# Two Sobel layers on shifted instead of normalized data, and weight centring moved into the attention

## The chip, the cores and the metric

The kernel runs on one core of a Trainium2 chip. The metric is the device time of one execution in microseconds (us), the median of several runs. A profile of one further execution gives the duration of every instruction on the core's engines: TensorE (PE in the profile, its weight loads PEld), VectorE (DVE), ScalarE (ACT), GpSimd (POOL) and SyncE (SP, which here issues transfers). Each engine works through its own queue in order; semaphores make it wait for the others.

## The reference

The input x has 256 rows, 256 columns and 32 channels, in float32. Four residual layers follow one another, each `x = x + layer(gn(x))`, where `gn` is a group norm with 16 groups of 2 channels over the whole image and no parameters.

- Layer 0: attention over an axis of length one, so that the softmax is 1 and only a layer norm, value and gate projections, their product and an output projection remain.
- Layers 1 and 2: a Sobel layer. `pooled` is the 3x3 mean of the normalized image, divided at the borders by the number of pixels that exist; `grad_x` and `grad_y` are the two 3x3 Sobel filters of it with zero padding; the result is `sqrt(grad_x^2 + grad_y^2 + 1e-6)`.
- Layer 3: a two-layer recurrent cell with group-normalized gates, which runs over the 256 columns, with the 256 rows as a batch.

For the change two facts count. A Sobel filter is linear and the group norm is `(x - mean) / deviation`, one mean and deviation per channel group. So the division may be done behind the filter, before or within the squares. The mean must be taken away ahead of it, since the zero padding makes the borders see it.

## The kernel before

**Layout.** The image lies in SBUF with 128 partitions = 4 columns x 32 channels, 64 blocks of 4 columns, 256 rows along the free axis. Work goes by pairs of blocks: `pair(t, k)` is 128 partitions x 512 elements, for k = 0 to 31. `xa` and `xb` are two such images; layer 1 reads `xa` and writes `xb`, layer 2 the reverse.

**Stages.** Input and transposes; group norm; layer norm; attention (L307 to L372); group norm (L376); first Sobel layer (L546); group norm (L548); second Sobel layer (L549); group norm and final weights (L559 to L561); the recurrence, which takes about three quarters of the time and has a plan of its own.

**Group norm** (L155). Per-partition means and variances of all pairs (`bn_stats`, L512, and `bn_aggr`, L158) are averaged over the partitions of a group by small products with a constant matrix; further products with a junk result (`busy`) keep TensorE at work meanwhile. A square root (L173), a reciprocal (L175) and one operation more (L177) give `scale` and `bias`.

**One pair in a Sobel layer.** A layer is a list of parts with due times, `every` apart from one pair to the next; all parts of all pairs are sorted by due time, and each engine gets its instructions in that order, with nothing reordered afterwards. The parts:

- `normalize` (L416): ScalarE writes scale * x + bias twice, into PSUM (`xp`) and SBUF (`xn`).
- `twos` (L423), `threes` (L432): VectorE adds neighbours along the rows, u[i] = xn[i] + xp[i+1], then pp = u[i] + xp[i+2]. `ends` (L426): ScalarE makes the two border values, 1.5 times u.
- `fours` (L437): VectorE, v = pp[i] + pp[i+1]. `difference` (L445): GpSimd, dh = pp[i] - pp[i+2]. `smooth` (L441): GpSimd, sh = v[i] + v[i+1]. dh and sh go into rings of 8 blocks (4 pairs).
- `centre` (L452, L462) and `edges` (L492): TensorE applies the filter across the columns. The centre is a product with the pair's own blocks, 128 rows and 128 columns of weights; the edges take one column from the block before and one from the block behind, with weights of 64 rows x 64 columns, into the two column halves. This is done for dh (`pg1`) and for sh (`pg0`). A float32 product shows as two records.
- `square` (L498) on ScalarE, twice; `total` (L502, ss) on VectorE; `root` (L506) on ScalarE; `residual` (L509) and `statistics` (L512) on VectorE.

The PSUM tiles `pg0` and `pg1` have three buffers each and `xp` two, eight banks in all. `pg1` holds dh's filter, then its square, then the root, until the residual has been added.

**Between the pairs.** Each `statistics` may be followed by one callback from a list. In layer 1 these are the centring steps of the recurrent weights (L634): `wc` and `bc` have their mean over each gate's 128 columns taken away, by reductions on VectorE (L644, L648) and subtractions on GpSimd (L651). In layer 2 they are five weight products (L658), which take a `pg1` buffer each. The loads of `wc`, `bc` and other weights are issued on SP's queue when `RecurrentWeights` is made, behind the attention (L374, L600 to L612).

**Attention.** For each of 32 pairs: eight value products and eight gate products on TensorE (L318), eight sigmoids on ScalarE (L333), eight multiplications on VectorE (L336), one `statistics` (L355), and a projection of eight products with 32 columns of weights each (L342), whose result GpSimd adds to the image (L352).

Of the kernel before, what the change touches and what calls it, by code (L numbers as in the profile page):

```python
# [61 lines left out]
def net_kernel(  # L62
# [120 lines left out]
    avg = big2.tile([P, KS, KS, J], F32, name="avg")  # L183
# [3 lines left out]
    spread = big2.tile([P, KS * J, C], F32, name="spread")  # L187
# [118 lines left out]

    stats = new_stats()  # L307
    with tc.tile_pool(name="at", bufs=3) as atp, tc.tile_pool(
# [48 lines left out]
        with tc.manual_schedule():  # L357
            together((), [(0, j) for j in range(J)])
            together((), [(1, j) for j in range(2)])
            for i in range(NST):  # L360
                for u in (2 * i, 2 * i + 1):
                    if i >= 3 and u % 2:
                        statistics(i - 3)
                    together([(u, 0), (u, 1)], [(u + 1, 2), (u + 1, 3)])
                    together([(u, 2), (u, 3)], [(u + 2, 0), (u + 2, 1)])
                if i >= 1:
                    project(i - 1)
            table(AF.Sqrt, one)
            for i in range(NST - 1, NST):
                project(i)  # L370
            for i in range(NST - 3, NST):
                statistics(i)  # L372
    lw = ctx.enter_context(tc.tile_pool(name="lw", bufs=1))
    rw = RecurrentWeights(tc, lw, ident, bout4, w_lat, b_lat, w_cell, b_cell, w_out)  # L374
    with tc.tile_pool(name="ps_gn", bufs=1, space=PSUM) as ps_gn:
        gn = group_norm(stats, ps_gn, 7, 12)  # L376
# [8 lines left out]
    def sobel_layer(src, dst, scale, bias, between):  # L385
# [24 lines left out]
        def normalize(k):  # L410
            for key, t in (
                ("xp", ps_c.tile([P, 2, S], F32, name="xp")),
                ("xn", sp.tile([P, 2, S], F32, name="xn")),
            ):
                v[key, k] = t
                nc.scalar.activation(  # L416
                    flat(t), pair(src, k), AF.Identity, scale=scale, bias=bias
                )

        def twos(k):  # L420
            u = v["u", k] = sp.tile([P, 2, S - 1], F32, name="u")
            xn, xp = v.pop(("xn", k)), v["xp", k]
            nc.vector.tensor_add(u, xn[:, :, 0 : S - 1], xp[:, :, 1:S])  # L423

        def ends(k):
            nc.scalar.mul(  # L426
                pps[k % 2][:, :, 1 : S + 1 : S - 1], v["u", k][:, :, 0 : S - 1 : S - 2], 1.5
            )

        def threes(k):  # L430
            u, xp = v.pop(("u", k)), v.pop(("xp", k))
            nc.vector.tensor_add(pps[k % 2][:, :, 2:S], u[:, :, 0 : S - 2], xp[:, :, 2:S])  # L432

        def fours(k):
            pp = pps[k % 2]
            w = v["v", k] = sp.tile([P, 2, S + 1], F32, name="v")
            nc.vector.tensor_add(w, pp[:, :, 0 : S + 1], pp[:, :, 1 : S + 2])  # L437
# [9 lines left out]
        def centre(k, which):  # L447
            pg = v["pg", which, k] = ps_s.tile([P, 2, S], F32, name=f"pg{which}")
            k0 = K_SOBEL + 5 * which
            b = 2 * k % RING  # L450
            if 0 < k < NST - 1:
                nc.tensor.matmul(  # L452
                    flat(pg),
                    lhsT=kt[:, k0 + 1, :],
                    rhs=flat(along[which][:, ring(k), :]),
                    start=True,
                    stop=False,
                )
                return
            for i in range(2):  # L460
                m = 3 if 2 * k + i == 0 else 4 if 2 * k + i == NB - 1 else 1
                nc.tensor.matmul(  # L462
                    pg[:, i, :],
                    lhsT=kt[:, k0 + m, :],
                    rhs=along[which][:, b + i, :],
                    start=i == 0,
                    stop=False,
                )

        def edges(k, which):  # L470

            pg = v["pg", which, k]
            k0 = K_SOBEL + 5 * which
            sides = []
            for m, first, rows, cols in (
                (0, 2 * k - 1, slice(Q, P), slice(0, Q)),
                (2, 2 * k + 1, slice(0, Q), slice(Q, P)),
            ):
                blocks = [(n, n - first) for n in (first, first + 1) if 0 <= n < NB]
                parts = []  # L480
                if len(blocks) == 2 and (first + 1) % RING:
                    b = first % RING
                    parts.append((flat(along[which][rows, b : b + 2, :]), flat(pg[cols])))
                else:
                    for n, i in blocks:
                        parts.append((along[which][rows, n % RING, :], pg[cols, i, :]))
                sides.append([(kt[rows, k0 + m, cols], rhs, out) for rhs, out in parts])
            while any(sides):
                for side in sides:
                    if side:  # L490
                        w, rhs, out = side.pop(0)
                        nc.tensor.matmul(out, lhsT=w, rhs=rhs, start=False, stop=not side)  # L492

        def square(k, which):
# [3 lines left out]
            nc.scalar.activation(sq, pg, AF.Square)  # L498
# [12 lines left out]
        def statistics(k):  # L511
            nc.vector.bn_stats(stats[:, k, :], pair(dst, k))  # L512

        every = 4.0
        parts = [
            (-1.45, normalize, ()),
            (0.0, twos, ()),
            (0.66, ends, ()),
            (0.66, threes, ()),
            (1.32, fours, ()),  # L520
            (1.4, difference, ()),
            (2.05, smooth, ()),
            (2.6 + 4.0, centre, (1,)),
            (3.46 + 4.0, centre, (0,)),
            (0.3 + 8.0, edges, (1,)),
            (1.35 + 8.0, edges, (0,)),
            (1.5 + 8.0, square, (1,)),
            (2.5 + 8.0, square, (0,)),
            (3.2 + 8.0, total, ()),
            (0.0 + 12.0, root, ()),  # L530
            (1.98 + 12.0, residual, ()),
            (2.6 + 12.0, statistics, ()),
# [5 lines left out]
        with tc.manual_schedule():  # L538
            for _, k, part, args in todo:
                part(k, *args)  # L540
                if part is statistics and between:
# [4 lines left out]
    stats = sobel_layer(xa, xb, *gn, rw.centring())  # L546
    with tc.tile_pool(name="ps_n", bufs=1, space=PSUM) as ps_n:
        gn = group_norm(stats, ps_n, 3, 12)  # L548
    stats = sobel_layer(xb, xa, *gn, rw.products())  # L549
# [41 lines left out]
class RecurrentWeights:  # L591


    def __init__(self, tc, lw, ident, bout4, w_lat, b_lat, w_cell, b_cell, w_out):
        self.nc = nc = tc.nc
        self.ident, self.bout4 = ident, bout4

        self.wc = lw.tile([P, L, 2, G], F32, name="wc")
        for l in range(L):
            nc.sync.dma_start(out=self.wc[:, l], in_=w_cell[l].rearrange("(k p) m -> p k m", p=P))  # L600
        self.wm = lw.tile([P, L * 2 * 4], F32, name="wm")

        self.bc = lw.tile([KX, L, G], F32, name="bc")
        nc.gpsimd.memset(self.bc, 0.0)
        nc.sync.dma_start(out=self.bc[C : C + 1], in_=b_cell.rearrange("(o l) m -> o l m", o=1))
        self.bm = lw.tile([KX, L * 4], F32, name="bm")

        self.lat = lw.tile([KX, H], F32, name="lat")
# [25 lines left out]
    def centring(self):  # L634
# [21 lines left out]
        return [lambda ps, p=out[i : i + 2]: [f() for f in p] for i in range(0, len(out), 2)]  # L656
# [441 lines left out]
```

## Time and profile before

| | us |
|---|---|
| median of 3 runs (2587.21 to 2589.66) | 2588.59 |
| the profiled execution | 2584.07 |
| its span, first to last instruction | 2582.1 |
| attention, about 107 to 320.8 | 213.8 |
| first Sobel layer, from L158 at 322.83 to L158 at 470.11 | 147.28 |
| second Sobel layer, to L158 at 615.72 | 145.61 |
| VectorE busy in the two layers | 130.87 and 127.64 |
| TensorE busy in the two layers | 142.50 and 140.16 |
| ScalarE busy in the two layers | 105.44 and 106.85 |
| GpSimd busy in the two layers | 96.05 and 82.55 |

In a line of the costliest groups, the line of the code, the engine and the operation are followed by `out<-in` with the names of the tiles, the shapes, the count, the busy time, the mean of one in ns, and behind the second bar the idle time of the engine just ahead of them with what ended it. In a line of the timeline stand the start and the duration in us, then the same names; a bracket at the end is the engine's idle time ahead of it and what ended it. Durations may overlap the next start by a little[...]; the distance of two starts is what an operation costs its queue.

### The profile page before, as it was taken

To read this page: it belongs to the slowest core of one execution; us is meant where nothing else is said; L and a number is where in the kernel's file an instruction comes from. 1 tells how busy PE (TensorE), PEld (TensorE's weight loads), DVE (VectorE), ACT (ScalarE), POOL (GpSimd) and SP (SyncE) were. 2 spreads that over 40 slices of the span, in tenths; PEclk is the share of its full clock that TensorE was granted. 3 is DMA by queue.
4 is the path that set the end of the run, shared out by engine and by line. 5 is a ranking of instruction groups with operands and counts; after the bars stand their busy time and mean duration, and the time that the engine had idled before them with its cause. 6 is when DMAs were issued, how large, how long until landed. Compare 5 with 4: busy or idle time off the path is not lost.

```text
span 2582.1 us, 40860 instructions
## 1 busy us (share of the span) xinstructions
PE 2530.7 (98%) x11181; PEld 1041.5 (40%) x11181; DVE 2317.7 (90%) x6735; ACT 2282.5 (88%) x6948; POOL 1284.0 (50%) x1292
## 2 busy tenths in 40 slices
PE   7999999998999999999999999999999999999997
PEld 4433333433344444444444444444444444444442
DVE  6788789896999999999999999999999999999997
ACT  5677667675999999999999999999999999999996
POOL 3211267563555555555555555555555555555553
PEclk9899999998999999999999999999999999999999
DMA  4000000002001001010101010100101010100000
GB/s 149 1 1 1 1 18 1 1 1 49 1 6 24 14 13 22 5 21 5 22 5 21 5 21 5 24 10 18 22 5 21 5 22 5 21 5 5 5 5 10
DMA packets 110870, 38.53 MB, mean 15 GB/s; under 512 B 74868, under 2 KB 107797, under 8 KB 110632
## 3 DMA queue, kind: packets, MB, share of 16 engines
q1 hardware_dynamic: 108452, 34.54, 6.2%
q8 instruction: 91, 1.49, 0.2%
q14 instruction: 147, 1.20, 0.2%
q10 hardware_dynamic: 1380, 0.99, 0.1%
q0 software_dynamic: 800, 0.30, 0.1%
HBM read 10.63 MB, written 8.39 MB: 7 GB/s over the span
## 4 chain that ended last, share of the span: by engine, by line
PE 94%; DVE 3%; ACT 1%; DMA 1%; POOL 0%; issue 0%; DVEq 0%; SPq 0%; ACTq 0%; POOLq 0%
PE zz L916 36%; PE zz L911 17%; PE zz L884 9%; PE pt L968 5%; PE pv L318 5%; PE pg L492 4%; PE pg L452 3%; PE zz L881 3%; PE pg L342 2%; PE pt L964 2%; PE px L1013 1%; PE pg L318 1%; PE pc L262 1%; PE px L1003 1%; PE pb L283 1%; DMA nat<-in_x_dram 1%
## 5 line engine op out<-in xcount | busy, mean ns | idle before, releaser
L932 POOL TENSOR_TENSOR rs<-ve,mhalf 128x4 f32<-128x4 f32 x1024 | 1032.1, 1008 | 921.9 <-DVE ve L929 921.9
L916 PE MATMUL zz<-wc,hT 128*128 128x512 f32 x2040 | 1058.6, 606 | 0.7 <-DVE hT L974 0.7
L905 ACT ACTIVATE ga<-zz,rs 128x128 f32<-128x128 f32 x3072 | 972.8, 377 | 39.2 <-POOL rs L932 9.7
L929 DVE TENSOR_REDUCE ve<-sq 128x4 f32<-128x516 f32 x1024 | 703.9, 687 | 27.9 <-ACT sq L924 7.1
L924 ACT ACTIVATE sq<-zz 128x512 f32<-128x512 f32 x1024 | 629.7, 615 | 37.0 <-PE zz L916 14.4
L911 PE MATMUL zz<-wc,hT 128*128 128x512 f32 x1024 | 524.2, 594 | 0.0
L916 PEld LDWEIGHTS zz<-wc,hT 128*128 128x128 f32 x2040 | 328.3, 190 | 398.1 <-DVE c L960 167.6
L905 ACT ACTIVATE go<-zz,rs 128x128 f32<-128x128 f32 x1024 | 394.0, 385 | 0.0
L952 DVE TENSOR_TENSOR c<-ga 128x128 f32<-128x128 f32 x1024 | 299.9, 293 | 62.0 <-ACT ga L905 40.3
L960 DVE TENSOR_TENSOR c<-c,fc 128x128 f32<-128x128 f32 x1020 | 288.4, 283 | 9.0
L956 DVE TENSOR_TENSOR fc<-ga,c 128x128 f32<-128x128 f32 x1020 | 292.5, 287 | 2.9 <-ACT ga L905 2.9
L884 PE MATMUL zz<-fx,xt 32*128 32x512 f32 x2048 | 265.7, 588 | 0.0
L336 DVE TENSOR_TENSOR o<-pv,sg 128x512 f32<-128x512 f32 x256 | 158.1, 681 | 42.4 <-PE pg L318 37.7
L968 PEld LDWEIGHTS pt<-ident,c 128*128 128x128 f32 x512 | 70.9, 139 | 285.5 <-DVE c L960 277.2
L971 ACT ACTIVATE th<-c 128x128 f32<-128x128 f32 x512 | 166.2, 325 | 0.4 <-DVE c L960 0.4
L333 ACT ACTIVATE sg<-pg 128x512 f32<-128x512 f32 x256 | 138.5, 599 | 30.7 <-PE pg L318 25.8
L971 ACT ACTIVATE th<-pt 128x128 f32<-128x128 f32 x512 | 146.0, 285 | 19.4 <-PE pt L968 19.4
L911 PEld LDWEIGHTS zz<-wc,hT 128*128 128x128 f32 x1024 | 161.0, 197 | 2.8 <-issue 0.5
L974 DVE TENSOR_TENSOR hT<-pt,th 128x128 f32<-128x128 f32 x512 | 146.3, 286 | 15.8 <-ACT th L971 15.7
L318 PE MATMUL pv<-xb,wv 32*128 32x512 f32 x512 | 156.2, 619 | 0.0
L980 DVE COPY hT<-pt 128x128 f32<-128x128 f32 x512 | 145.5, 284 | 8.9 <-PE pt L968 8.8
L964 PEld LDWEIGHTS pt<-ident,go 128*128 128x128 f32 x512 | 71.5, 140 | 202.9 <-ACT go L905 202.9
(169 smaller groups left out, 2986.6 us busy)
## 6 DMA issues: line engine op xcount, KB each, us to landing
xt<-xa SPq DMA_DIRECT2D x256, 64.0 KB, 2.0
nat<-in_x_dram SPq DMA_DIRECT2D x16, 512.0 KB, 7.9
out_dram<-st SPq DMA_DIRECT2D x252, 32.0 KB, 1.7
wc<-in_L_conv_W_cell_dram SPq DMA_DIRECT2D x2, 512.0 KB, 4.6
kt<-in_consts_dram ACTq DMA_DIRECT2D x1, 704.0 KB, 7.0
kg<-in_consts_dram ACTq DMA_DIRECT2D x1, 128.0 KB
wv<-in_L_conv_Wv_dram POOLq DMA_DIRECT2D x4, 32.0 KB, 5.4
wg<-in_L_conv_Wg_dram POOLq DMA_DIRECT2D x4, 32.0 KB, 6.4
```

What stands on the lines that cost most here:

```text
L318: nc.tensor.matmul(ps, lhsT=w[rows, half * P : (half + 1) * P], rhs=mn, start=True, stop=True)
L884: nc.tensor.matmul(v["zz", l, h, t], lhsT=inputs.of(t, r), rhs=fx[r, :], start=False, stop=l == 0 and t == 0,)
L905: nc.scalar.activation(dst, gates(x, g), func, scale=scale)
L911: nc.tensor.matmul(get("zz"), lhsT=v["hT", 0, t][:, seqs], rhs=wc[:, l, 0, :], start=False, stop=t == 0)
L916: nc.tensor.matmul(get("zz"), lhsT=v["hT", l, t - 1][:, seqs], rhs=wc[:, l, 1, :], start=False, stop=True,)
L924: nc.scalar.activation(sqs[l, h, t % 2][:, :, 0:H], four(get("zz")), AF.Square, scale=float(H**-0.5))
L929: nc.vector.tensor_reduce(ve, sqs[l, h, t % 2], AX.X, ALU.add)
L932: nc.gpsimd.tensor_tensor(rs, get("ve"), inputs.mhalf, ALU.pow)
L952: nc.vector.tensor_mul(c, gates(get("ga"), 0), gates(get("ga"), 2))
L956: nc.vector.tensor_mul(fc, gates(get("ga"), 1), get("c"))
L960: nc.vector.tensor_add(c, c, get("fc"))
L971: nc.scalar.activation(th, get("pt")[:, 1, 0:P] if turned else get("c"), AF.Tanh)
```

## The change

- `normalize` becomes `convert`: ScalarE writes x - 1.5 mean into `xp` alone, and `twos` adds the plain `src` to it. A sum of one plain value and two such values is a sum of three less 3 means. `ends` has -0.75 mean as bias. `scale` and its reciprocal are made by `deviation`, behind the first `twos`, and go into `square` as a scale.
- `fours` moves from VectorE to GpSimd.
- `centre` and `edges` become `mixed`: for each column half, products with all 128 rows of weights and 64 columns, one for the pair's own blocks and one for the neighbours; the two halves alternate.
- All due times are new; `every` goes from 4.0 to 3.44.
- The group norm ahead of a Sobel layer moves into the layer (`shift`), with 16 junk products behind its last small product instead of 12.
- The loads of `wc` and `bc` are issued ahead of the attention, once the tiles `avg` and `spread`, now in a pool of their own, are free. The 32 centring steps are emitted one behind each pair of the attention instead of two behind each of the first 16 pairs of layer 1. The remaining weights are loaded as before (`rest`).

```diff
+    means.close()
+    cells = ctx.enter_context(tc.tile_pool(name="cells", bufs=1))
+    rw = RecurrentWeights(tc, cells, w_cell, b_cell)
+    centring = rw.centring()
...
                 if i >= 1:
                     project(i - 1)
+                if centring:
+                    centring.pop(0)()
...
-    def sobel_layer(src, dst, scale, bias, between):
+    def sobel_layer(src, dst, moments, before, after, between):
...
-        def normalize(k):
-            for key, t in (
-                ("xp", ps_c.tile([P, 2, S], F32, name="xp")),
-                ("xn", sp.tile([P, 2, S], F32, name="xn")),
-            ):
-                v[key, k] = t
-                nc.scalar.activation(
-                    flat(t), pair(src, k), AF.Identity, scale=scale, bias=bias
-                )
+        def shift():
...
+            nc.vector.bn_aggr(mv, moments)
+            busy(before)
+            nc.tensor.matmul(pm[:, 0:1], lhsT=kg[:, K_GN, :], rhs=mv[:, 0:1], start=True, stop=True)
+            busy(2)
+            nc.scalar.mul(m15, pm[:, 0:1], -1.5)
+            nc.scalar.mul(m75, pm[:, 0:1], -0.75)
...
+            nc.tensor.matmul(pm[:, 1:2], lhsT=kg[:, K_GN, :], rhs=q, start=True, stop=True)
+            busy(after)
+
+        def deviation():
+            nc.scalar.activation(std, v.pop("pm")[:, 1:2], AF.Sqrt, bias=gn_eps)
+            nc.vector.reciprocal(scale, std)
+
+        def convert(k):
+            xp = v["xp", k] = ps_c.tile([P, 2, S], F32, name="xp")
+            nc.scalar.activation(flat(xp), pair(src, k), AF.Identity, bias=m15)
 
         def twos(k):
             u = v["u", k] = sp.tile([P, 2, S - 1], F32, name="u")
-            xn, xp = v.pop(("xn", k)), v["xp", k]
-            nc.vector.tensor_add(u, xn[:, :, 0 : S - 1], xp[:, :, 1:S])
+            nc.vector.tensor_add(
+                u, src[:, 2 * k : 2 * k + 2, 0 : S - 1], v["xp", k][:, :, 1:S]
+            )
...
-            nc.vector.tensor_add(w, pp[:, :, 0 : S + 1], pp[:, :, 1 : S + 2])
+            nc.gpsimd.tensor_add(w, pp[:, :, 0 : S + 1], pp[:, :, 1 : S + 2])
...
+        def mixed(k, which):
+
             pg = v["pg", which, k] = ps_s.tile([P, 2, S], F32, name=f"pg{which}")
             k0 = K_SOBEL + 5 * which
...
+            for side in range(2):
+                cols = slice(side * Q, (side + 1) * Q)
                 parts = []
...
+                for d in (side - 1, side):
+                    m = 1 + d
+                    blocks = [n for n in (2 * k + d, 2 * k + 1 + d) if 0 <= n < NB]
+                    whole = len(blocks) == 2 and (blocks[0] + 1) % RING
+                    if whole and (d or 0 < k < NST - 1):
+                        b = blocks[0] % RING
+                        parts.append((kt[:, k0 + m, cols], flat(along[which][:, b : b + 2, :]), flat(pg[cols])))
+                        continue
...
             while any(sides):
-                for side in sides:
+                for i, side in enumerate(sides):
                     if side:
-                        w, rhs, out = side.pop(0)
-                        nc.tensor.matmul(out, lhsT=w, rhs=rhs, start=False, stop=not side)
+                        w, rhs, dst = side.pop(0)
+                        first = len(side) == count[i] - 1
+                        nc.tensor.matmul(dst, lhsT=w, rhs=rhs, start=first, stop=not side)
...
-            nc.scalar.activation(sq, pg, AF.Square)
+            nc.scalar.activation(sq, pg, AF.Square, scale=scale)
...
-        every = 4.0
+        every = 3.44
         parts = [
-            (-1.45, normalize, ()),
-            (0.0, twos, ()),
-            (0.66, ends, ()),
-            (0.66, threes, ()),
-            (1.32, fours, ()),
-            (1.4, difference, ()),
-            (2.05, smooth, ()),
-            (2.6 + 4.0, centre, (1,)),
-            (3.46 + 4.0, centre, (0,)),
-            (0.3 + 8.0, edges, (1,)),
-            (1.35 + 8.0, edges, (0,)),
-            (1.5 + 8.0, square, (1,)),
-            (2.5 + 8.0, square, (0,)),
-            (3.2 + 8.0, total, ()),
-            (0.0 + 12.0, root, ()),
-            (1.98 + 12.0, residual, ()),
-            (2.6 + 12.0, statistics, ()),
+            (-0.72, convert, ()),
+            (0.00, twos, ()),
+            (2.77, threes, ()),
+            (2.77, ends, ()),
+            (4.40, fours, ()),
+            (5.57, difference, ()),
+            (7.15, smooth, ()),
+            (10.90, mixed, (1,)),
+            (11.97, square, (1,)),
+            (12.75, mixed, (0,)),
+            (12.85, square, (0,)),
+            (14.29, total, ()),
+            (14.79, root, ()),
+            (16.34, residual, ()),
+            (17.10, statistics, ()),
         ]
...
-    stats = sobel_layer(xa, xb, *gn, rw.centring())
...
-    stats = sobel_layer(xb, xa, *gn, rw.products())
+    stats = sobel_layer(xa, xb, stats, 7, 16, [])
+    stats = sobel_layer(xb, xa, stats, 3, 16, rw.products())
```

## The prediction

> **What bounds the kernel now.** I first cut the span into stages by the moments at which statistics are aggregated (L158): the attention ends near 320.8 us, the first Sobel layer runs from 322.83 to 470.11 (147.28 us), the second from there to 615.72 (145.61 us), and what follows, the recurrence, isn't touched. The chain of waits is almost all TensorE (94%), which misleads for the Sobel layers, so I read them from the queues. VectorE's timeline over one step of the first layer (columns: start, duration, engine, line, operation):
>
> ```profile
> 424.37 0.68 DVE L423 TENSOR_TENSOR u<-xn,xp 128x510 f32<-128x510 f32 x1
> 425.16 0.68 DVE L432 TENSOR_TENSOR pp<-u,xp 128x508 f32<-128x508 f32 x1
> 425.97 0.69 DVE L437 TENSOR_TENSOR v<-pp 128x514 f32<-128x514 f32 x1
> 426.58 0.68 DVE L509 TENSOR_TENSOR xb<-xa,pg 128x512 f32<-128x512 f32 x1
> 427.30 0.69 DVE L512 BATCH_NORM_STATS2 stats<-xb 128x6 f32<-128x512 f32 x1
> 427.91 0.67 DVE L502 TENSOR_TENSOR ss<-sq,pg 128x512 f32<-128x512 f32 x1
> 428.50 0.68 DVE L423 TENSOR_TENSOR u<-xn,xp 128x510 f32<-128x510 f32 x1
> ```
>
> Six operations, no idle time in brackets: VectorE sets the step of 4.13 us, the distance of the two u rows. The starts show more than the durations: an operation that reads what the one before it wrote starts 0.72 to 0.81 us after it (u to pp 0.79, pp to v 0.81, xb to stats 0.72), an independent one after 0.59 to 0.61 (v to xb, stats to ss, ss to u).
>
> Next, the other engines. TensorE, where it runs freely (339.17, 340.13, 341.08, 341.99, then 342.94), gives 0.96, 0.95, 0.91 and 0.95 to the four parts of a pair: 3.77 us. ScalarE waits 0.86 us each step for L502. GpSimd has one slow row and one that tells why:
>
> ```profile
> L445 POOL TENSOR_TENSOR dh<-pp 128x512 f32<-128x512 f32 x64 | 98.7, 1542 | 100.0 <-DVE pp L432 75.3 <-ACT xp L416 15.5 <-ACT pg L498 4.7
> L441 POOL TENSOR_TENSOR sh<-v 128x512 f32<-128x512 f32 x64 | 66.3, 1036 | 0.0
> ```
> ```profile
> 393.02 1.55 POOL L445 TENSOR_TENSOR dh<-pp 128x512 f32<-128x512 f32 x1 [0.41 <-DVE pp L432]
> 397.45 1.25 POOL L445 TENSOR_TENSOR dh<-pp 128x512 f32<-128x512 f32 x1 [0.71 <-DVE pp L432]
> 401.27 1.55 POOL L445 TENSOR_TENSOR dh<-pp 128x512 f32<-128x512 f32 x1 [0.41 <-DVE pp L432]
> ```
>
> The difference takes 1.55 us where it runs 0.66 us beside VectorE's v (L437), the one operation with both inputs in SBUF, and 1.25 where, started late, it shares only 0.36 us with it. That leaves 1.03, what sh takes.
>
> Last, the tail of the first layer, where nothing lies between the sum, the root and the residual:
>
> ```profile
> 463.67 0.67 DVE L502 TENSOR_TENSOR ss<-sq,pg 128x512 f32<-128x512 f32 x1
> 465.10 0.69 DVE L509 TENSOR_TENSOR xb<-xa,pg 128x512 f32<-128x512 f32 x1 [0.76 <-ACT pg L506]
> 465.82 0.69 DVE L512 BATCH_NORM_STATS2 stats<-xb 128x6 f32<-128x512 f32 x1
> ```
>
> From ss to xb VectorE needs 1.43 us, 0.76 of them idle. In the steady step above it had u, pp and v to do there.
>
> **The change part by part.** *VectorE loses v.* By starts that is 0.81 us of 4.13. But the new order matters more than the count. The due times, modulo 3.44, give VectorE: u(n) 0.00, ss(n-4) 0.53, xb(n-4) 2.58, pp(n) 2.77, stats(n-4) 3.34. ss and xb are now neighbours, and the root stands between them. An engine works through its queue in order, so the 1.43 us of the tail come into every step: u to ss 0.60, ss to xb 1.43, xb to pp 0.61, pp to stats 0.60, stats to u 0.61, together 3.85 us. If nothing else is slower, the step goes from 4.13 to 3.85, not to the 3.44 written in the code.
>
> *ScalarE* loses xn (0.80 us). Its queue is root(n-4), square 1 and square 0 of n-3, convert(n+1), ends(n). A second loop runs through it: ss to root 0.72, root to square 0.65, square to square 0.52, to convert 0.48, convert to u 0.80 (duration 0.77 and the hand-over), u to ss 0.60: 3.77. Just under 3.85, so hidden; it is what comes next if VectorE's loop were shorter.
>
> *GpSimd* gains fours (514 elements, two inputs). The Trainium skill speaks against this (GPSIMD Engine Reference, § 4.1 Engine selection): elementwise additions belong on VectorE, GpSimd being some 2x slower. By that rule, three times twice the 0.70 of v, GpSimd would need 4.2 us per step and set the pace, giving back the gain and 4 us more. The rows say less: 1.04 for sh, and dh falls to 1.03 since v no longer runs on VectorE (the page's § 1, contention with two SBUF inputs, agrees with the 1.25 row). I take 3 x 1.04 = 3.1; with dh left at 1.55 it is 3.6; with L352's in-place 1.27 for fours, 3.3. All below 3.85.
>
> *TensorE*: eight 128x64x512 products instead of two full and four quarter ones. L342's sixteen records on four column tiles take four slots of 0.43 us (weight loads at 316.26, 316.69, 317.12), so column tiles run side by side; two at a time, 16 records take 8 slots: 3.42 us. If the changes of tile shape cost the 0.35 us between that and 3.77 (TensorEngine Tiling (Array Packing), § Key Properties, says a change of mode drains the array), they are gone; otherwise 3.77 remains. Neither reaches 3.85.
>
> *Step and fill.* I follow the queues from the aggregation, t = 0. Mean ready 1.50 (as 322.83 to 324.33), m15 and m75 0.4, convert 0.77, so u(0) at 2.75 instead of 4.89; the deviation follows beside it. In the fill GpSimd counts: three operations per pair from 4.3, dh(1) ends at 9.4, sh(1) at 10.4, then the last product 0.9, square 0.6. Square 0 of pair 0 stands ahead of convert(4) in ScalarE's queue: u(4) at 12.7, ss(0) at 13.3. Then 27 steps of 3.85 to ss(27) at 117.25. Behind it pp(31) ends at 2.73, the three GpSimd operations at 5.86, four products 1.7 us each at 10.9, square, sum, root, residual, statistics 3.6: 14.5. A layer is 131.75 us. The first saves 147.28 - 131.75 = 15.5. The second has the weight products between its steps; today their steps (4.9, 4.73, 4.71, 4.35, 4.67) exceed 4.13 by 2.7 in all, and since two sums of 0.66, their waits and four copies (0.72) now fall into tighter loops, I put 2.5: 145.61 - 134.25 = 11.4.
>
> *Centring moves into the attention.* One of 32 steps behind each pair: six reductions (0.67 each) and two scalings on VectorE, 24 subtractions (0.60) on GpSimd. The place is just behind four gated products, where VectorE idles 1.22 us of 6.69 for TensorE:
>
> ```profile
> 225.31 2.48 DVE L336 TENSOR_TENSOR o<-pv,sg 128x512 f32<-128x512 f32 x4 [1.22 <-PE pg L318]
> ```
>
> So a reduction is hidden, and costs 0.6 where the gap is missing: at the first pair only, where sixteen products run without a gap (106.89 for 9.65 us). With no cover at all it would be 8 x 0.6 = 5. Its loads leave SP's empty queue near 103 us; the first reduction, and all gated products queued behind it, would wait for them if they took over 8 us (wc landed in 4.6). GpSimd's 1.27 + 0.60 per 6.69 us is free. I take +0.6.
>
> Sum: -15.5 - 11.4 + 0.6 = -26.3 us. The profiled execution took 2584.07 (span 2582.1), which becomes 2557.8; the median of the runs is 4.5 higher, 2588.59, and becomes 2562.3.
>
> **The rivals.** 54 steady steps (27 per layer) convert a step into time.
> (a) TensorE sets the step at 3.43 to 3.6: the plan's 3.44 comes true. Against it stands the order of ss and xb. It gives 54 x 0.42 = 23 less: 2540.
> (b) GpSimd paces: dh stays 1.55 and fours takes the same, 1.55 + 1.55 + 1.04 = 4.14. The 1.25 row speaks against it. 54 x 0.29 = 16 more: 2578.
> (c) The other side: the column halves don't run side by side, being two products that read the same rows. Then a pair takes 8 x 0.85 = 6.8 us of TensorE, and each layer some 30 x 2.95 = 89 more: 2740. L342 shows four tiles side by side, but with different inputs. It decides from a step of 3.85 + 26.3/54 = 4.34 on.
> (d) The reductions aren't hidden, or the clock halves in other places: TensorE's granted clock is at half between about 614 and 621 and again between 631 and 638 us, behind 3 us without a product at the end of the second layer; 5 us at most: 2567, or as much less.
>
> **How the numbers follow.** The step of 3.85 has 0.70 (with (d) in it: 2553 to 2571, from 0.1 us on each of 54 steps and 3 for fill and clock), (a) and mixtures below 3.75 0.12, (b) and steps of 4.0 to 4.3 0.13, (c) and its like beyond 4.34 0.05. The range reaches most of the way to (a) and (b), 2543 to 2575. Within 0.2% (5 us, about what a measurement of this kernel can tell) needs a step of about 4.25 to 4.43: 0.02. Faster 0.93, slower 0.05.
>
> **What would show it.** In the changed profile: u to u of 3.85 us in both layers, VectorE idle about 0.75 us ahead of xb, put down to the root; dh near 1.03; records of L517 in 8 slots of 0.43 us; layers near 132 and 134 us; an attention within 1 us of before. A step of 3.44 with no idle ahead of xb, or GpSimd without gaps, makes me wrong.

## The result, and the profile after

The changed kernel takes 2563.18 us, the median of 4 runs (2561.91 to 2570.22), against 2588.22 (2587.21 to 2589.66) for the kernel before beside it: a ratio of 0.991, 95% interval 0.9893 to 0.9926. That is faster by 0.9%, more than the 0.2% that a measurement of this kernel can tell. The forecast was 2562.3, in a range of 2543 to 2575.

The profiled execution took 2562.2 us (span 2560.4; before 2584.07 and 2582.1), 21.7 us less of span. Cut at the aggregations of the statistics, it goes like this:

| stretch | before, us | after, us | difference | forecast |
|---|---|---|---|---|
| start to the first aggregation | 322.83 | 322.65 | -0.2 | +0.6 |
| first Sobel layer | 147.28 | 133.25 | -14.0 | -15.5 |
| second Sobel layer | 145.61 | 135.70 | -9.9 | -11.4 |
| recurrence and what lies around it | 1966.4 | 1968.8 | +2.4 | 0 |

The first row holds more than the attention: the first gated product starts at 106.89 before and at 106.09 after, and in the kernels below, which have the code of the changed kernel ahead of it, anywhere from 105.88 to 108.91. From there to the aggregation it is 215.94 and 216.56, so the attention itself pays the 0.6 of the forecast.

The busy times of the two layers after, by the stretches of the trace (columns: stretch, its length, busy time of TensorE, its weight loads, VectorE, ScalarE and GpSimd, granted clock, DMA share, GB/s):

```profile
322.65:455.90 133.25, 126.62 (x633) 60.07 (x632) 101.02 (x169) 86.79 (x163) 97.35 (x98) 1.00 0.01 1
455.90:591.60 135.70, 128.57 (x638) 62.73 (x637) 102.08 (x167) 87.62 (x168) 98.41 (x108) 1.00 0.03 7
```

Only TensorE looks near full, at 95% of the first layer, and that deceives: a kernel below (both_orders) does the same products in a layer of 122.82 us. What sets the step must again be read from the queues. VectorE's timeline after, one step (columns as in the prediction: start, duration, engine, line, operation, and in brackets the idle time before it with what ended it):

```profile
425.27 0.67 DVE L455 TENSOR_TENSOR u<-xa,xp 128x510 f32<-128x510 f32 x1
425.85 0.68 DVE L527 TENSOR_TENSOR ss<-sq,pg 128x512 f32<-128x512 f32 x1
427.29 0.69 DVE L534 TENSOR_TENSOR xb<-xa,pg 128x512 f32<-128x512 f32 x1 [0.76 <-ACT pg L531]
427.90 0.68 DVE L470 TENSOR_TENSOR pp<-u,xp 128x508 f32<-128x508 f32 x1
428.49 0.69 DVE L537 BATCH_NORM_STATS2 stats<-xb 128x6 f32<-128x512 f32 x1
429.09 0.67 DVE L455 TENSOR_TENSOR u<-xa,xp 128x510 f32<-128x510 f32 x1
```

From u to u it is 3.82 us, where the kernel before had 4.13; 0.76 of them are idle ahead of xb (L534), for the root (L531). That is the 1.43 us of the old tail, now in every step, as forecast. There is no idle time ahead of u, so by this view the convert is always there in time. ScalarE's timeline over the same stretch says how narrowly:

```profile
426.57 0.69 ACT L531 ACTIVATE pg<-ss,sobel_eps 128x512 f32<-128x512 f32 x1 [1.15 <-DVE ss L527]
427.20 0.64 ACT L523 ACTIVATE pg<-pg,scale 128x512 f32<-128x512 f32 x1
427.77 0.68 ACT L523 ACTIVATE sq<-pg,scale 128x512 f32<-128x512 f32 x1
428.34 0.69 ACT L451 ACTIVATE xp<-xa,m 128x512 f32<-128x512 f32 x1
428.95 0.29 ACT L460 ACTIVATE pp<-u,m 128x4 f32<-128x4 f32 x1
```

The convert (L451) starts at 428.34, and u takes its output at 429.09. The second loop of the prediction is here: ss to root 0.72, root to square 0.63, square to square 0.57, to the convert 0.57, to u 0.75, u to ss 0.59. That is 3.83, not the 3.77 of the forecast: the two loops are equal to 0.01 us.

TensorE, when it has its data, needs 1.72 us for one `mixed`, that is for four products or eight records (128*64 is the shape of the tile; the last row lacks a record):

```profile
426.39 2.27 PE L517 MATMUL pg<-dh,kt 128*64 128x512 f32 x8
428.12 2.26 PE L517 MATMUL pg<-sh,kt 128*64 128x512 f32 x8
429.83 2.22 PE L517 MATMUL pg<-dh,kt 128*64 128x512 f32 x7
```

Eight records in 1.72 us are four slots of 0.43: two column halves run at a time (at the start of the layer two records begin together at 334.91 and again at 335.34), and a pair takes 3.44.

GpSimd's groups in the two layers (columns: line, operation, count, busy us and mean ns, idle us before them and what ended it):

```profile
L475 POOL TENSOR_TENSOR v<-pp 128x514 f32<-128x514 f32 x64 | 66.9, 1045 | 56.5 <-ACT pp L460 42.6 <-DVE pp L470 11.8 <-PE pg L517 1.4
L483 POOL TENSOR_TENSOR dh<-pp 128x512 f32<-128x512 f32 x64 | 66.7, 1041 | 0.0
L479 POOL TENSOR_TENSOR sh<-v 128x512 f32<-128x512 f32 x64 | 66.6, 1041 | 0.0
```

The difference (dh) has come down from 1542 to 1041 ns, and the three additions start 1.00 us apart, so GpSimd works for 3.0 us of each step and waits for the rest.

### The profile page after: what moved, and what is told of

Read it like the earlier page. It is cut to its first block, busy times and chain, and to the rows that moved or that the text cites. A ratio compares the mean times of both kernels' runs of the same rounds, so it can differ in the third digit from the quotient of the medians.

```text
span 2560.4 us, 41317 instructions
## 1 busy us (share of the span) xinstructions
PE 2506.6 (98%) x11469; PEld 1048.9 (41%) x11469; DVE 2266.8 (89%) x6667; ACT 2247.8 (88%) x6888; POOL 1315.4 (51%) x1356
## 4 chain that ended last, share of the span: by engine, by line
PE 88%; DVE 6%; ACT 2%; issue 2%; DMA 1%; POOL 0%; SPq 0%; POOLq 0%; DVEq 0%; ACTq 0%
PE zz L941 36%; PE zz L936 17%; PE zz L909 9%; PE pt L993 5%; PE pv L324 5%; PE zz L906 3%; PE pg L348 2%; PE pt L989 2%; PE pg L517 2%; ACT pg L531 1%; PE px L1038 1%; DVE pp L470 1%; PE pg L324 1%; DVE ss L527 1%; DVE u L455 1%
## 5 line engine op out<-in xcount | busy, mean ns | idle before, releaser
L930 ACT ACTIVATE ga<-zz,rs 128x128 f32<-128x128 f32 x3072 | 975.6, 378 | 38.7 <-POOL rs L957 10.2
L954 DVE TENSOR_REDUCE ve<-sq 128x4 f32<-128x516 f32 x1024 | 705.0, 688 | 29.5 <-ACT sq L949 8.5
L517 PE MATMUL pg<-dh,kt 128*64 128x512 f32 (+1 forms) x584 | 156.5, 542 | 7.4 <-POOL dh L483 6.3
```

The costliest lines, as they stand in the source:

```text
L930: nc.scalar.activation(dst, gates(x, g), func, scale=scale)
L954: nc.vector.tensor_reduce(ve, sqs[l, h, t % 2], AX.X, ALU.add)
```

## The experiments

Twelve kernels follow; each ratio is against the kernel before on the same chip. The steps and layers come from each kernel's own profiled execution. They are edits of the changed kernel, except centring_alone, which is one of the kernel before; none leaves out any of the computation. Extra work, where there is some, is named.

My theory: VectorE's loop over the root holds the step at 3.83, with ScalarE's loop directly under it; GpSimd and TensorE have slack. The rivals: GpSimd paces; TensorE does; or it is the removal of an operation, not the order, that gave the time.

### The two loops, one at a time and together

**xb_later** moves the residual behind pp and so lets VectorE work while the root runs.

```diff
-            (16.34, residual, ()),
+            (16.60, residual, ()),
```

> Residual (xb) due at 16.60 instead of 16.34: pp(n) now stands between ss(n-4) and xb(n-4) on VectorE. VectorE's loop becomes 0.59 + 1.43 + 0.72 + 0.60 = 3.34 us. Theory 1 (VectorE's ss - root - xb loop alone sets the step of 3.83): the step falls to TensorE's 3.43, 54 x 0.40 = 21 us less, near 2542. Theory 2 (a second loop of the same length runs through ScalarE: ss to root 0.72, root to square 0.63, square to square 0.57, to convert 0.57, convert to u 0.75, u to ss 0.59 = 3.83): the step stays 3.82 to 3.83, and the time near 2563.

**convert_early** takes the convert and the ends ahead of the squares in ScalarE's queue.

```diff
-            (-0.72, convert, ()),
+            (-2.34, convert, ()),
-            (2.77, ends, ()),
+            (1.15, ends, ()),
```

> Convert and ends of the next pairs due ahead of the squares in ScalarE's queue; VectorE's order as in the changed kernel. Both theories: VectorE's loop of 3.83 us stays and the step with it, near 2563; the fill is shorter by up to 2 us per layer, since convert(4) no longer waits for square 0 of pair 0, so 2559 to 2563. If the step falls below 3.7, VectorE's loop was not a bound.

**both_orders** makes both edits.

> Both edits. VectorE's loop 3.34, ScalarE's loop without convert about 3.25, GpSimd 3.1, TensorE's eight slots 3.42 to 3.45. Theory 2: only this one gets the step to TensorE's 3.43 to 3.5, 54 x 0.35 to 0.40 = 19 to 21 us less than the changed kernel, near 2542 to 2545. Theory 1: the same time as with the residual alone moved.

| kernel | median, us | ratio (95%) | steady step | first, second layer |
|---|---|---|---|---|
| before, same chip | 2591.02 | 1 | | |
| xb_later | 2560.53 | 0.9885 (0.9869 to 0.9902) | 3.81 | 132.79, 134.92 |
| convert_early | 2559.60 | 0.9884 (0.9868 to 0.9901) | 3.83 | 131.74, 134.04 |
| both_orders | 2544.86 | 0.9824 (0.9808 to 0.9841) | 3.44 | 122.82, 128.90 |

(Around the start of the second layer TensorE's granted clock is at half for 3.4 us in convert_early and for 6.8 us in both_orders, and not in xb_later.) Each edit alone leaves the step within 0.02 us of where it was; together they shorten it by 0.39. That is the mark of two loops of the same length, and neither GpSimd nor TensorE was touched. With the residual moved, VectorE's timeline shows which loop holds:

```profile
424.69 0.69 DVE L455 TENSOR_TENSOR u<-xa,xp 128x510 f32<-128x510 f32 x1 [0.35 <-ACT xp L451]
425.30 0.68 DVE L527 TENSOR_TENSOR ss<-sq,pg 128x512 f32<-128x512 f32 x1
425.90 0.68 DVE L470 TENSOR_TENSOR pp<-u,xp 128x508 f32<-128x508 f32 x1
426.74 0.69 DVE L534 TENSOR_TENSOR xb<-xa,pg 128x512 f32<-128x512 f32 x1 [0.16 <-ACT pg L531]
```

The wait ahead of xb has fallen from 0.76 to 0.16 us, and a new one of 0.35 stands ahead of u, for the convert (L451). With convert_early it is the other way about: 0.76 ahead of xb, none ahead of u. In both_orders only the 0.16 is left:

```profile
395.93 0.69 DVE L527 TENSOR_TENSOR ss<-sq,pg 128x512 f32<-128x512 f32 x1
396.54 0.68 DVE L470 TENSOR_TENSOR pp<-u,xp 128x508 f32<-128x508 f32 x1
397.38 0.69 DVE L534 TENSOR_TENSOR xb<-xa,pg 128x512 f32<-128x512 f32 x1 [0.16 <-ACT pg L531]
398.10 0.69 DVE L537 BATCH_NORM_STATS2 stats<-xb 128x6 f32<-128x512 f32 x1
398.71 0.67 DVE L455 TENSOR_TENSOR u<-xa,xp 128x510 f32<-128x510 f32 x1
```

The 3.44 of this step is that of TensorE, whose products follow one another without a gap at 1.72 us each, two per pair; VectorE's own loop (ss to xb 1.45, to stats 0.72, to u 0.61, to ss 0.60) would allow 3.38. So the step of rival (a) is there to be had, by three changed due times.

### The second sums, and GpSimd's slack

**sums_on_vector** puts the second sums (v) back on VectorE and keeps the new order.

```diff
-            nc.gpsimd.tensor_add(w, pp[:, :, 0 : S + 1], pp[:, :, 1 : S + 2])
+            nc.vector.tensor_add(w, pp[:, :, 0 : S + 1], pp[:, :, 1 : S + 2])
```

> Fours back on VectorE, all else as in the changed kernel. Its due time (4.40, modulo 3.44 0.96) puts v(n-1) into the gap between ss and xb, where VectorE idles 0.76 us for the root. If the step is set by the hand-over to the root, v costs nothing there: step 3.83 to 3.85, dh back to 1.5 where it meets v, and the fill some 2 us shorter per layer: 2559 to 2564. If the move of the second sums to GpSimd is what shortened the step (count of VectorE's work), the step grows by 0.6: 54 x 0.6 = 32 us more, near 2595.

It took 2563.71 us (before there 2591.02), ratio 0.9894 (0.9878 to 0.9911), step 3.83, first layer 132.92. VectorE's timeline:

```profile
424.82 0.68 DVE L527 TENSOR_TENSOR ss<-sq,pg 128x512 f32<-128x512 f32 x1
425.42 0.69 DVE L475 TENSOR_TENSOR v<-pp 128x514 f32<-128x514 f32 x1
426.26 0.69 DVE L534 TENSOR_TENSOR xb<-xa,pg 128x512 f32<-128x512 f32 x1 [0.15 <-ACT pg L531]
```

The sum v fits into the gap ahead of xb and leaves 0.15 us of it. So taking v from VectorE bought nothing in the shipped order. The step before had the same six operations on VectorE and needed 4.13, since three of them read what stood directly before them (0.79, 0.81, 0.72 instead of 0.60). What shortened the step is the order in which the queue holds them, not their number. In this kernel dh also takes 1.04: v now runs at another time than dh (0.08 us of overlap in this step), and what made dh slow before was the overlap, as the rows of 1.55 and 1.25 had said.

**difference_twice** computes dh twice on GpSimd, one piece of extra work per pair.

```diff
-            nc.gpsimd.tensor_sub(along[1][:, ring(k), :], pp[:, :, 0:S], pp[:, :, 2 : S + 2])
+            for _ in range(2):
+                nc.gpsimd.tensor_sub(along[1][:, ring(k), :], pp[:, :, 0:S], pp[:, :, 2 : S + 2])
```

> The changed kernel with GpSimd's difference done twice (same result): four operations of 1.00 us by their starts per pair, 4.0 us, over the step of 3.83. GpSimd becomes the bound: step 4.0 to 4.1, 54 x 0.2 to 0.25 = 11 to 14 us more, and the fill, which GpSimd sets, longer by some 3 us per layer: 2578 to 2584. If GpSimd had more slack than its starts show, less than 5 us more.

It took 2585.29 us (2583.13 to 2589.52; before there 2588.08), ratio 0.999 (0.9981 to 0.9999). GpSimd's timeline has no gap left:

```profile
424.81 1.04 POOL L479 TENSOR_TENSOR sh<-v 128x512 f32<-128x512 f32 x1
425.81 1.04 POOL L475 TENSOR_TENSOR v<-pp 128x514 f32<-128x514 f32 x1
426.81 2.16 POOL L484 TENSOR_TENSOR dh<-pp 128x512 f32<-128x512 f32 x2
428.92 1.04 POOL L479 TENSOR_TENSOR sh<-v 128x512 f32<-128x512 f32 x1
```

The step becomes 4.11, GpSimd's own 4 operations, and the layers 144.09 and 147.20. That is the step of rival (b), 4.14, made on purpose: 1.1 us more on GpSimd moved it by 0.28, so 0.8 of them went into slack. The time is 7 us above what I gave to that rival. There I had left out that a layer's start and end also wait for four GpSimd operations per pair instead of three: in the first layer u(4) comes 1.0 us later, and from the last u to the aggregation it is 17.68 us here and 15.33 in the changed kernel. The expectation of this run had 3 us per layer for it, and the time is 1.3 above that.

**convert_twice** adds a second copy on ScalarE behind the convert, which nobody reads, in place of the xn that the change removed.

```diff
             nc.scalar.activation(flat(xp), pair(src, k), AF.Identity, bias=m15)
+            xn = sp.tile([P, 2, S], F32, name="xn")
+            nc.scalar.activation(flat(xn), pair(src, k), AF.Identity, bias=m15)
```

> The changed kernel with a second copy of each pair written by ScalarE behind convert, as the kernel before had it (into SBUF, read by nobody, so it is pure queue time). It stands between convert and the next root but not between convert and u: the loop ss - root - squares - convert - u - ss doesn't hold it, but ScalarE's own queue and the order root behind ends do. If u starts when the first copy is done, the ends and the copy fill ScalarE beside u and ss: ScalarE's queue needs 0.63 + 0.57 + 0.57 + 0.61 + 0.70 + 0.29 = 3.4 plus the wait of the root for ss; between convert and root then lie 0.61 + 0.70 + 0.29 = 1.6 instead of 0.75 + 0.59 + 0.72 = 2.06 today: still covered, step 3.83, time 2563 to 2566. If instead the number of ScalarE operations sets the step, it grows by 0.7: 54 x 0.7 = 38 us more, near 2601.

It took 2566.13 us (2564.03 to 2568.94), ratio 0.9916 (0.9898 to 0.9933); the step is 3.83 and the first layer 133.85. The root's wait falls from 1.15 to 0.54 us, which is where the copy went. So the missing xn gives nothing to the step either. At the start of a layer it is another matter: the first u came 4.89 us into the layer before and comes at 2.49 now, where it takes the data as they are and a convert that needs the mean alone.

### The column halves

**old_products** gives the changed kernel the products of before, full centre and four quarter edges, but at each of its two due times one after the other: centre and edges of one kind, then of the other (centre and edges themselves are word for word those of before).

```diff
         def mixed(k, which):
...
+            centre(k, which)
+            edges(k, which)
```

> The changed kernel with the filter's products as before it: one product with all 128 columns for the centre and 64x64 products for the edges, at the due times of mixed. TensorE then needs the 3.77 us per pair seen in the kernel before, still under the step of 3.83: step 3.83 to 3.85, time near 2563, so the column halves alone are worth nothing in the changed kernel. If TensorE already limits at times, up to 5 us more.

**both_old_products** does so in both_orders.

> As before, with both orders mended (the run of 2544.9 us, step 3.43). If the column halves save the 0.35 us per pair between 3.77 and 3.42, the step is 3.77 to 3.80 here and the time 54 x 0.34 = 18 us more, near 2563. If 3.77 was only a pace set from outside, the step stays 3.43 to 3.5 and the time near 2545 to 2548.

Both missed: 2588.72 us, ratio 1.0007 (0.9998 to 1.0016), and 2589.18, ratio 1.0004 (0.9995 to 1.0013), the speed of the kernel before. TensorE's timeline in old_products (columns as above; x counts records, and starts of consecutive rows give the time of a part):

```profile
421.16 1.08 PE L530 MATMUL pg<-dh,kt 64*64 64x512 f32 x4
422.17 1.13 PE L490 MATMUL pg<-sh,kt 128*128 128x512 f32 x2
423.22 1.08 PE L530 MATMUL pg<-sh,kt 64*64 64x512 f32 x4
424.23 1.12 PE L490 MATMUL pg<-dh,kt 128*128 128x512 f32 x2
425.28 1.07 PE L530 MATMUL pg<-dh,kt 64*64 64x512 f32 x4
```

The parts take 1.01, 1.05, 1.01 and 1.05 us, 4.12 in all, not the 3.77 that I had taken over from before. I had changed more than I meant: the tile's shape changes four times per pair here, between 128x128 and 64x64, and twice in the kernel before, where both centres come first and both edges after. Two further kernels keep that order.

**grouped_products** is the changed kernel with centre, centre, edges, edges; **both_grouped_products** has the same in both_orders.

```diff
         def mixed(k, which):
...
+            if which:
+                centre(k, 1)
+                centre(k, 0)
+            edges(k, which)
```

> The changed kernel with the old products, but in the old order: centre of dh, centre of sh, edges of dh, edges of sh, two changes of tile shape per pair instead of the four of the run with old products, where TensorE needed 4.13 us per pair. If a change of shape costs (4.13 - 3.42) / 4 = 0.18 us, TensorE needs 3.42 + 0.36 = 3.78 here, under the loops of 3.83: step 3.83 to 3.86 and, with the tail longer by some 1 us per layer, 2563 to 2568. If products with 64 rows are slow by themselves, the step stays at 4.1 and the time near 2588.

> The same with both orders mended. By 0.18 us per change of shape TensorE's 3.78 us set the step: 54 x 0.34 = 18 us over the 2544.9 of the run with both orders, near 2563 to 2567. If changes of shape cost nothing when TensorE has no data to wait for, the step is 3.43 and the time near 2545.

```profile
421.30 1.12 PE L490 MATMUL pg<-dh,kt 128*128 128x512 f32 x2
422.27 1.02 PE L490 MATMUL pg<-sh,kt 128*128 128x512 f32 x2
423.22 1.08 PE L530 MATMUL pg<-dh,kt 64*64 64x512 f32 x6
424.13 1.03 PE L530 MATMUL pg<-sh,kt 64*64 64x512 f32 x6
425.09 1.12 PE L490 MATMUL pg<-dh,kt 128*128 128x512 f32 x2
```

These rows are of both_grouped_products: 0.97, 0.95, 0.91, 0.96, 3.79 in all, and its step is 3.78. grouped_products took 2563.23 us (before there 2586.08), ratio 0.9917 (0.99 to 0.9933), with the step of 3.83 that the loops give: in the shipped order the column halves are worth nothing that these runs can tell. both_grouped_products took 2564.91, ratio 0.9929 (0.9912 to 0.9946), where both_orders had 2544.86 and 0.9824: once both loops are mended, the column halves are worth 19 us by the two profiles' layers (134.23 + 136.64 against 122.82 + 128.90, where only both_orders has a half clock, 6.8 us around the start of its second layer) and 20 by the medians, which are of two chips.

With 0, 2 and 4 changes of shape a pair takes 3.43, 3.77 and 4.13 us, so some 0.18 us per change. It is an even count, but not a proof of the place: in the grouped order all four parts are longer than 0.86 us, which is half of the 1.72 of a `mixed`, also those at which no shape changes, and in old_products each edge product also adds to the tile that the product just before it wrote (the column halves add to their own tiles too, at no extra time). Shape and accumulation were not separated by a run.

### The centring, and the clock

**centring_alone** is the kernel before with one part of the change, the centring of the recurrent weights among the attention's steps (the reading of weights and the 32 small parts of it, taken word for word from the changed kernel).

```diff
+    rw = RecurrentWeights(tc, cells, w_cell, b_cell)
+    centring = rw.centring()
...
                     project(i - 1)
+                if centring:
+                    centring.pop(0)()
...
-    stats = sobel_layer(xa, xb, *gn, rw.centring())
+    stats = sobel_layer(xa, xb, *gn, [])
```

> The kernel before, with the centring of the weights and their loads moved into the attention and nothing else. The steps of the first layer with centring between them exceed 4.13 by 1.2 + 0.6 + 0.6 + 1.2 + 0.8 = 4.4 us (5.32, 4.72, 4.72, 5.31, 4.92); these go, and the attention gets up to 0.6: 4 us less than before. If the attention pays for eight more VectorE operations, 1 us more than before.

It took 2582.16 us (2578.46 to 2586.91; before there 2586.08), ratio 0.9984 (0.9977 to 0.9991). The first layer is 142.94 us, 4.3 less, with all its steps from the fourth on at 4.12 or 4.13 where five had been 4.7 to 5.3. Of the changed kernel's gain in the first layer, about 4 of 14 us come from there.

**both_warm** is both_orders with seven more products into an unused bank behind the last product of each Sobel layer: extra work that nobody reads, meant to leave TensorE no gap of 3 us while the last square, root and residual run.

```diff
                 part(k, *args)
+                if part is mixed and k == NST - 1 and args == (0,):
+                    warm = ps_c.tile([P, 2, S], F32, name="xp")
+                    for _ in range(7):
+                        nc.tensor.matmul(warm[:, 0, :], lhsT=ident, rhs=kg, start=True, stop=True)
```

> Both orders mended, and seven junk products of 0.43 us behind the last product of each Sobel layer, into a free bank, so that TensorE isn't idle for 3 us while the last pair goes through squares, sum, root and residual. If these gaps are what halves TensorE's granted clock at the start of the following group norm, the small products there take 2 to 4 us less per layer end and the weights' products too: 2 to 6 us less than 2544.9. If the clock halves anyway, the same time.

TensorE behind the second layer, in the changed kernel and then in both_warm:

```profile
590.98 2.90 PE L148 MATMUL junk<-kg,ident 128*128 128x256 f32 x6 [3.12 <-DVE xa L534]
593.67 0.42 PE L161 MATMUL pm<-mv,kg 128*128 128x1 f32 x2
```
```profile
569.09 3.29 PE L568 MATMUL xp<-kg,ident 128*128 128x256 f32 x14
572.27 1.53 PE L148 MATMUL junk<-kg,ident 128*128 128x256 f32 x6
```

The same three junk products (six records) take 2.90 us behind a gap of 3.12 and 1.53 where the seven (fourteen records) stand ahead of them. The granted clock was at half from 444.9 to 451.8, from 574.7 to 578.1 and from 591.7 to 602.0 in both_orders; in both_warm only 588.4 to 598.6 is left. The second layer goes from 128.90 to 126.38, its first u coming 2.48 instead of 3.53 us behind the aggregation, and what follows from 1965.9 to 1965.1. Its median is 2539.95 us (2539.85 to 2540.07), ratio 0.9828 (0.9812 to 0.9845). The kernel before was at 2586.08 there and at 2591.02 beside both_orders, so by the ratios the two are equal, and the 3 us less rest on one profile each. Nor does every such gap bring the half clock: the first layer of the changed kernel ends with a gap of 3.12 as well, and the three junk products behind it take 1.53. So what these seven products are worth is left open; that both_orders and both_warm beat both kernels isn't, with ratios of 0.9824 and 0.9828 where the changed kernel has 0.991.

## Why the prediction was right, and where its steps were off

**VectorE's loop of 3.85.** Right, and for the reason given: 3.83, with the root's gap of 0.76 in each step. convert_early shows this loop alone still at 3.83.

**ScalarE's second loop, "3.77 ... just under 3.85, so hidden".** The loop is there, link by link, but mis-sized by 0.06 us: square to square is 0.57 instead of 0.52, the last square to the convert 0.57 instead of 0.48, and the convert to u 0.75 instead of 0.80. I had read these distances from the kernel before, where the squares had no scale and the convert had one. It cost the forecast nothing in time. It did hide that the two loops are one limit: by 3.77, mending VectorE's order alone should give 54 x 0.06 = 3 us, and by the step of xb_later, 3.81, it gives 1.

**GpSimd 3.1.** Right: 3 x 1.04, 1.00 by starts. But the working behind dh's 1.03 doesn't come out: 1.55 us with 0.66 of overlap and 1.25 with 0.36 give 0.89 without any, if the cost grows in step with the overlap. The 1.03 was that of sh, and 1.04 came. Of the two prices the row was right and the rule of the Trainium skill (GPSIMD Engine Reference, § 4.1 Engine selection) too dear: 1.04 against VectorE's 0.69 is 1.5 times, not 2. Where the rule would have decided is seen in difference_twice, at 4.11 us per step. Yet sums_on_vector says that the move bought nothing either: I had named "VectorE loses v" as the first part of the change, and put the order second as what "matters more". Only the second carried the gain of the step.

**TensorE 3.42 or 3.77, "neither reaches 3.85".** Right, and the 0.35 us of which I left open whether they go with the shapes did go: 3.43. The halves run side by side, so rival (c) is out. That the Trainium skill says that a change of mode drains the array (TensorEngine Tiling (Array Packing), § Key Properties) fits 3.43, 3.77 and 4.13, with the reserve told above.

**Fill and tail.** The start was better than forecast, u(0) at 2.49 us instead of 2.75. But u(4) came at 14.62 instead of 12.7. The step that failed is "the last product 0.9": I let the first pair's difference product be done before sh(1) was there. In the trace dh(1) is there 9.17 us into the layer, TensorE leaves its junk products and starts pair 0 at 9.62 (332.27), and it is 3.7 us more until the second square can start. The junk products alone hold this start: in sums_on_vector dh(1) is there at 7.84, and pair 0 still starts at 9.61 and u(4) comes at 14.62. ScalarE's square shows what it waits for (5.09 us, then 1.06, each ended by a product):

```profile
334.25 0.66 ACT L523 ACTIVATE pg<-pg,scale 128x512 f32<-128x512 f32 x1 [5.09 <-PE pg L517]
335.97 0.69 ACT L523 ACTIVATE sq<-pg,scale 128x512 f32<-128x512 f32 x1 [1.06 <-PE pg L517]
336.55 0.68 ACT L451 ACTIVATE xp<-xa,m 128x512 f32<-128x512 f32 x1
```

Against the forecast u(4) is 1.92 later, the 27 steps are 0.65 shorter and the tail 0.23 longer: 133.25 instead of 131.75. The second layer is 2.45 longer than the first, where 2.5 was put for the weight products.

**The attention, + 0.6.** Right, and for the reason given. From the first gated product to the aggregation it is 0.62 us longer (215.94 to 216.56), with VectorE 3.7 us busier and GpSimd 13.7. The first pair pays it, where the reduction meets no gap:

```profile
106.09 4.88 DVE L342 TENSOR_TENSOR o<-pv,sg 128x512 f32<-128x512 f32 x8 [5.09 <-PE pv L324]
110.88 0.67 DVE L669 TENSOR_REDUCE bm<-bc 33x4 f32<-33x512 f32 x1
111.48 4.86 DVE L342 TENSOR_TENSOR o<-pv,sg 128x512 f32<-128x512 f32 x8
```

The other reductions are hidden. All twelve kernels of the experiments, which have the centring in the same place, take 216.48 to 216.61 us for this stretch.

**What wasn't in the sum.** Behind the second layer the changed kernel has the half clock for 6.8 + 13.7 us, before for 6.8 + 6.8, and this stretch is 2.4 us longer; 1.65 of them are there at the 22nd variance of the recurrence (L929 before, L954 after), 59.81 and 61.46 us behind the aggregation. Rival (d) had named the place and its size. The layers are 2.9 longer than forecast and the last stretch 2.4, less 0.8 ahead of the attention and 0.2 around the span: 4.3 of the 4.4 us by which the profiled 2562.2 lies above the 2557.8. The median lies only 0.9 above its forecast, since this time the profiled execution was 1 us below the median where it had been 4.5 below: part of the exact hit is chance.

**The gain, by parts.** In the first layer, between the same u rows of both traces: the start 2.4 us, the first four steps 3.0, the centring that stood between the later steps 3.1, 27 steps shorter by 0.30 each 8.1, less 2.6 for the longer way from the last u to the aggregation; together 14.0. Of the 3.0 of the first four steps 1.2 are centring too (they take 15.13 us before, 13.94 in centring_alone and 12.13 after), which with the 3.1 makes the 4.3 measured alone. The shorter step is put down to the order of the queues because it stays at 3.83 when v, a copy or the old products in their old order are put back, each alone; no run puts all three back, or gives the kernel before the new due times and nothing else. How the gain of the start divides between the missing deviation and the missing xn, and where the other 1.8 us of the first four steps come from, no run here tells.

## What to carry to other kernels

Read a software pipeline as loops through several queues: an operation and the one that waits for another engine's answer to it should not be neighbours in an in-order queue, and a loop that is as long as the longest to a few hundredths of a microsecond has to be shortened with it, or next to nothing is gained. Work taken off an engine that idles in its loop was worth nothing to the step here, and work put into its idle time cost the step nothing, whatever the share of busy time says. When a part is to be undone for an experiment, keep its place in the queue and its neighbours: the same products in another order cost 0.35 us per pair of TensorE's time here.

## What was not expected of the hardware

- The fp32 products of a pair take 3.43, 3.77 or 4.13 us by their order and tile shapes (0, 2 or 4 changes between 128x128 and 64x64).
- A square on ScalarE with a scale held per partition starts 0.57 us ahead of the next operation, one without 0.52 (0.64 to 0.68 and 0.58 us long). That is where a part of the second loop's 0.06 came from.
- At gaps of 3.0 to 3.9 us on TensorE the granted clock was at half for 3.4, 6.8, 10.2 or 13.7 us, in some places and executions and not in others.
